# A conditioned block kernel: the opening's first slot tile reordered, slot transposes in two accumulators, the last half tile in quarters

## The chip, the cores and the metric

The kernel runs on one core of one Trainium2 chip. A core has TensorE (matmuls, here PE, with its weight loads as PEld), VectorE (DVE), ScalarE (ACT), GpSimd (POOL) and SyncE (SP, which issues most of the DMAs). The metric is the device time in microseconds of one execution, as the median of several. A profile of one execution shows when each instruction ran, on which engine, from which line of the kernel.

## The reference

The input x has 32 batch rows of 128 tokens with 512 features, in float32. A vector t per batch row (512 values) gives six modulation vectors through two linear layers after a SiLU: shift, scale and gate for each half. m marks the masked tokens, a few of each batch row.

```python
norm = _layernorm(x) * (1.0 + scale[:, None]) + shift[:, None]
norm = jnp.where(m, norm, 0.0)
fwd = _ssm_fallback(norm, ssm_w1, ssm_b1, ssm_w2, ssm_b2)
bwd = jnp.flip(_ssm_fallback(jnp.flip(norm, axis=1), bwd_w1, bwd_b1, bwd_w2, bwd_b2), axis=1)
x = x + gate_msa[:, None] * jnp.where(m, fwd + bwd, 0.0)
ff_norm = _layernorm(x) * (1.0 + scale_mlp[:, None]) + shift_mlp[:, None]
return x + gate_mlp[:, None] * (gelu(ff_norm @ ff_w1 + ff_b1) @ ff_w2 + ff_b2)
```

The first half (`_ssm_fallback` is two linear layers with an exact gelu between) matters only for the tokens that m marks. The second half is a feed-forward layer, 512 to 1024 to 512, for all tokens.

## The kernel before

**First half.** The marked tokens are gathered into 512 slots, four tiles of 128 (0 to 3). `slots_to_count` (lines 250 to 255) and `counted` (257 to 270) turn the mask into token numbers: TensorE multiplies a pick matrix with ranks, DVE compares and sums. Tiles 0 and 1 are gathered early by POOL, tiles 2 and 3 later (`gather_slots`, 289). `pm_ss` (628) receives the shift and scale rows of all batch rows from 32 matmul records as `ada_w` arrives; `modulation_rows` (318) copies them to `mod1` with DVE. `of_slots` (322 to 341) then forms the rows of each slot: four strips of 128 features, each in a PSUM accumulator of its own, with matmuls that use 32 rows of the array. Before, one call (634) makes the strips of tiles 0 and 1 in the same four accumulators. `modulated_by_strips` (343 to 354) normalises a slot tile with four DVE instructions for mean and scale, and four for the root and the shift. `transposed_slots` (189 to 196) transposes the tile by four TensorE transposes into one accumulator and two ScalarE copies of half each; it is called for slot tile 0 (682), tile 1 (691), and, back to back, tiles 2 and 3 (828 to 829). `hidden_of_tile` (666 to 680, matmuls at line 673) is the first layer for one tile and `hidden` (198) for two; `gates_of_slots` (356) makes the gate strips, and `project` (214, matmuls at 221) is the second layer.

**PSUM accumulators.** They come from three pools that reuse their buffers in turn: `ps_t` (tag "tr", two), `ps_h` (tag "h", three), `ps_o` (tag "o", three). A new tile waits until the last reader of the one two (or three) allocations back is done.

**Order.** From line 436 on the order on every engine is that in which the program issues its instructions; nothing reorders them. TensorE also multiplies things that nobody reads, into `pm_keep_clock`, to stay busy: `keep_clock(2, 0)` (635) and two matmuls on the first tile's scaled rows (646 to 649).

**Loads.** SP issues the weights and the raw x tiles in one queue: `ada_w` first, then `ssm_w1`, `bwd_w1`, two x tiles (`load_raw`, 599), `ssm_w2`, `ff_w1` and the rest. DVE takes statistics of the raw x tiles (`own_statistics`, 166) between the slot work, from line 778.

**Second half.** `FirstProduct` and `SecondProduct` do the feed-forward layer with seven products of half-size blocks in place of eight, over four pairs of 4 + 4 batch rows. The last step of the last pair (`SecondProduct.step`, 1286 to 1345, branch `last`) makes the last half of the last output tile: two token blocks (i) of 128 rows by 256 columns, each with its four matmuls into a "tr" accumulator, a multiplication by the gate and an addition to x on DVE, and a store by SP. After it come only the tests whether more slots are needed (1573 on; the loop behind them isn't entered with these inputs) and the final waits.

Of the kernel before, what the change touches and what calls it, by code (L numbers as in the profile page):

```python
# [9 lines left out]
F32 = mybir.dt.float32  # L10
# [12 lines left out]
def kernel(  # L23
# [49 lines left out]
    nc = tc.nc  # L73
    B, S, D = x.shape
    P = 128
    assert S == P
    G = 4
    NP = B // (2 * G)
    KC = D // P
# [3 lines left out]
    NH = NS // 2  # L83
    NC = NS // P
# [104 lines left out]
    def transposed_slots(xn, dst, name):  # L189

        ptr = ps_t.tile([P, 512], F32, tag="tr", name=f"ptr_{name}")
        for k in range(KC):
            nc.tensor.transpose(ptr[:, ts(k, P)], xn[:, ts(k, P)], ident)
        for half_no in range(2):
            k = ts(half_no, KC // 2)
            nc.scalar.copy(dst[:, k], ptr.rearrange("p (k s) -> p k s", s=P)[:, k])
# [53 lines left out]
    def slots_to_count(picked, n, name, bank):  # L250

        pl = bank[0].tile([P, 512], F32, tag=bank[1], name=f"pl_{name}")
        for c in range(n):
            nc.tensor.matmul(pl[:, ts(c, S)], picked[:B, ts(c, P)], rank, start=True, stop=True)  # L254
        return pl[:, : n * S].rearrange("p (c s) -> p c s", s=S)
# [28 lines left out]
    xc = []  # L284
# [33 lines left out]
    def modulation_rows(pm, mod, lo, hi):  # L318
        view = pm[:, : (hi - lo) * P].rearrange("p (m c) -> p m c", c=P)
        nc.vector.tensor_copy(mod[:, lo:hi], view)  # L320
# [140 lines left out]
    for j, op in enumerate((ALU.is_gt, ALU.is_ge)):  # L461
        nc.gpsimd.affine_select(
            out=upper[:, j],
# [167 lines left out]
    slots_of_late = slots_to_count(pick[:, NH:], NC // 2, "s1", (ps_h, "h"))  # L631
    modulation_rows(pm, mod1, 0, 2)

    strips = of_slots(pick, (0, 1), mod1, slice(0, 2), 3 * [(ps_o, "o")] + [(ps_h, "h")], "part_s0")
    keep_clock(2, 0)
# [4 lines left out]
    for c in range(2):  # L640
        mv, rstd = statistics(xc[c : c + 1], f"s{c}")
        xn_s.append(
            modulated_by_strips(xc[c], strips, c, xn[:, c], mv[:, 0, 0:1], rstd, xn[:, 2 + c])
        )
        if c == 0:
            for n in range(2):
                nc.tensor.matmul(
                    pm_keep_clock[:, ts(n, 2 * P)], ident, xn[:, 2, ts(n, 2 * P)], start=True, stop=True
                )
            token_i = counted(slots_of_late, slot_col[:, NC // 2 :], NC // 2, "s1", ssm)  # L650
# [31 lines left out]
    transposed_slots(xn_s[0], xT_s[:, :, ts(0, P)], "s0")  # L682
# [542 lines left out]
    class SecondProduct:  # L1225
# [60 lines left out]
        def step(self, step, late=False):  # L1286
# [12 lines left out]
            for i in range(2):  # L1299
                part = bank[:, ts(i, D // 2)]  # L1300
                if last:
                    part = ps_t.tile([P, 512], F32, tag="tr", name=f"last_{i}")[:, : D // 2]
                for k in range(hh):
                    nc.tensor.matmul(  # L1304
                        part,
                        src[:, k, ts(i, P)],
                        w[product][:, k, :],
                        start=(last and k == 0),
                        stop=True,
                        skip_group_check=True,  # L1310
                    )
                if last:

                    t = tp.tile([P, D // 2], F32, tag="t", name=f"t_last_{i}")
                    gate = self.gate[1][:, 2 * c + i, : D // 2]
                    nc.vector.tensor_tensor(t, part, gate, ALU.mult)
                    xt = self.xs[1][c][:, i, : D // 2]
                    nc.vector.tensor_tensor(xt, xt, t, ALU.add)
                    nc.sync.dma_start(out[(2 * p + 1) * G + 2 * c + i, :, : D // 2], xt)
# [371 lines left out]
```

## Time and profile before

| | before |
|---|---|
| median of 3 runs | 456.0 us (455.75 to 456.08) |
| the profiled execution's own time | 455.45 us |
| span of the profile | 453.7 us |
| TensorE busy | 446.6 us, 98% |
| VectorE busy | 331.7 us, 73% |
| ScalarE busy | 178.0 us, 39% |
| GpSimd busy | 159.8 us, 35% |
| mean granted TensorE clock | 0.999 |

The span runs from the first to the last instruction; the profiled execution's own time has 1.75 us around it. In a line of the timeline stand the start, the duration, the engine, the line of the kernel, the operation, output<-inputs, the number of instructions merged into the line, and in brackets how long the engine stood idle before and what released it. A float32 matmul appears as two records. The ends of matmuls are modelled, since they overlap in the array.

### The profile page before, as it was taken

How to read it: one execution, taken by the hardware profiler on the slowest of the kernel's cores; microseconds unless marked ns; L12 is line 12 of the kernel's file. 1: busy time of each engine (PE TensorE's matmuls, PEld its weight loads, DVE VectorE, ACT ScalarE, POOL GpSimd, SP SyncE). 2: the span in 40 equal slices, each digit the busy share in tenths (PEclk: the TensorE clock that was granted, in tenths of full speed). 3: DMA queues.
4: the chain of work that ended last, by engine and by line, in shares of the span. 5: the costliest groups of instructions: out<-in, count | busy, mean ns of one | idle time of the engine just before them, and what ended most of it. 6: DMA issues, size and time to landing. Idle time of an engine off the chain costs nothing.

```text
span 453.7 us, 6170 instructions
## 1 busy us (share of the span) xinstructions
PE 446.6 (98%) x2151; PEld 370.4 (82%) x2151; DVE 331.7 (73%) x571; ACT 178.0 (39%) x390; POOL 159.8 (35%) x154
## 2 busy tenths in 40 slices
PE   8999999999999999999999999999999999999996
PEld 3884585688888888888888888888888888888885
DVE  5798797697789759886796498867963995534645
ACT  3124127244642552446425514454355154552000
POOL 4220550089770000797700007977000027560000
PEclk9999999999999999999999999999999999999999
DMA  7999449745518817722187167221872442222023
GB/s 251 379 396 407 150 73 326 279 151 172 189 78 180 114 49 251 249 92 82 66 191 107 56 230 264 95 84 54 202 105 59 157 145 82 81 94 93 0 82 107
DMA packets 82611, 70.57 MB, mean 156 GB/s; under 512 B 63112, under 2 KB 63728, under 8 KB 81554
## 3 DMA queue, kind: packets, MB, share of 16 engines
q1 hardware_dynamic: 67762, 58.28, 40.9%
q0 software_dynamic: 4160, 10.54, 6.9%
q10 hardware_dynamic: 10656, 1.33, 2.1%
q8 instruction: 18, 0.29, 0.2%
q14 instruction: 15, 0.12, 0.1%
HBM read 56.46 MB, written 13.70 MB: 155 GB/s over the span
## 4 chain that ended last, share of the span: by engine, by line
PE 92%; DVE 5%; POOL 1%; issue 1%; ACT 1%; DVEq 0%
PE a_o L1304 23%; PE a_m L1117 18%; PE e_o L1304 18%; PE e_m L1117 14%; PE po_s L221 6%; PE ph_s L204 5%; PE ph_s L673 2%; PE pm_ss L309 1%; PE last L1304 1%; PE pm_f L309 1%; PE a_m_alone L1117 1%; PE pl_s L254 1%; DVE xn_sy L1050 0%; PE part_s L333 0%; DVE e_m L1142 0%
## 5 line engine op out<-in xcount | busy, mean ns | idle before, releaser
L1168 POOL TENSOR_TENSOR ha<-p_m,ha 128x512 f32<-128x512 f32 x20 | 25.8, 1289 | 178.8 <-ACT ha L1175 169.2
L1304 PE MATMUL e_o<-fw,ha 128*128 128x256 f32 x256 | 57.9, 379 | 0.0
L939 ACT ACTIVATE xT<-xT,modT 128x128 f32<-128x128 f32 x112 | 44.1, 480 | 31.6 <-DMA xT<-xn 31.4
L1304 PE MATMUL a_o<-t,hb 128*128 128x256 f32 x240 | 54.1, 379 | 0.0
L1304 PEld LDWEIGHTS e_o<-fw,ha 128*128 128x128 f32 x256 | 48.6, 190 | 6.6
L1304 PEld LDWEIGHTS a_o<-t,hb 128*128 128x128 f32 x240 | 45.6, 190 | 6.2
L1079 ACT ACTIVATE hb<-hb,biasT 128x256 f32<-128x256 f32 x64 | 29.0, 500 | 30.4 <-POOL hb L1201 19.8
L1131 ACT COPY p_m<-e_m 128x512 f32<-128x512 f32 x27 | 15.8, 586 | 47.8 <-PE e_m L1117 43.3
L885 POOL DMA_INDIRECT x<-x_rows,slot_i x24 | 29.2, 1218 | 6.0 <-issue 5.3
L1168 POOL TENSOR_TENSOR hb<-p_m,hb 128x512 f32<-128x512 f32 x20 | 29.6, 1481 | 0.3
L1304 PE MATMUL a_o<-fw,ha 128*128 128x256 f32 x128 | 28.9, 379 | 0.0
L1304 PE MATMUL a_o<-t,s 128*128 128x256 f32 x128 | 28.9, 379 | 0.0
L1304 PE MATMUL e_o<-fw,s 128*128 128x256 f32 x128 | 28.9, 379 | 0.0
L221 PE MATMUL po_s<-w,h_s 128*128 128x512 f32 x64 | 28.4, 594 | 0.0
L1175 ACT COPY ha<-e_m 128x512 f32<-128x512 f32 x32 | 18.5, 578 | 24.9 <-PE e_m L1117 24.6
L1304 PEld LDWEIGHTS a_o<-t,s 128*128 128x128 f32 x128 | 24.3, 190 | 3.3
L1304 PEld LDWEIGHTS a_o<-fw,ha 128*128 128x128 f32 x128 | 24.3, 190 | 3.3
L1304 PEld LDWEIGHTS e_o<-fw,s 128*128 128x128 f32 x128 | 24.3, 190 | 3.3
L1142 DVE TENSOR_TENSOR e_m<-a_m,ha 128x512 f32<-128x512 f32 x20 | 13.9, 696 | 17.0 <-POOL ha L1168 6.6
L1079 ACT ACTIVATE ha<-e_m,biasT 128x256 f32<-128x256 f32 x48 | 20.0, 468 | 14.8 <-PE e_m L1117 12.6
L1117 PE MATMUL a_m<-xT,tw 128*128 128x256 f32 x96 | 24.7, 380 | 0.4 <-DVE hb L1147 0.4
L1117 PE MATMUL e_m<-s,fw 128*128 128x256 f32 x92 | 23.8, 381 | 0.0
(237 smaller groups left out, 892.3 us busy)
## 6 DMA issues: line engine op xcount, KB each, us to landing
tw<-t_rows SPq DMA_DIRECT2D x16, 896.0 KB, 5.3
x<-in_x_dram SPq DMA_DIRECT2D x16, 512.0 KB, 8.8
gate<-gate_rows POOLq DMA_DIRECT2D x8, 1024.0 KB, 5.2
out_dram<-x SPq DMA_DIRECT2D x15, 512.0 KB, 4.9
xT<-xn SPq DMA_DIRECT2D x92, 64.0 KB, 2.4
ada_f<-in_L_cond_ffada_w_dram SPq DMA_DIRECT2D x4, 768.0 KB, 13.2
ada_a<-in_L_cond_ada_w_dram SPq DMA_DIRECT2D x4, 512.0 KB
w<-in_L_cond_ssm_w_dram SPq DMA_DIRECT2D x2, 1024.0 KB, 6.2
```

Source lines behind the costliest of these rows:

```text
L204: nc.tensor.matmul(ph[:, :n], w[:, k, ts(f, P)], xT[:, k, :], start=(k == 0), stop=(k == KC - 1))
L221: nc.tensor.matmul(po, h[f][:, ts(i, P)], w[:, f, :], start=(f == 0 and seeded is None), stop=(f == HC - 1), skip_group_check=seeded is no ...
L309: nc.tensor.matmul(pm[ts(j, B), : (hi - lo) * P], sT[:, k, :], kinds[:, k, lo:hi, ts(j, P)], start=False, stop=True, skip_group_check=True,)
L885: nc.gpsimd.indirect_dma_start(out=xs[i // G][i % G // 2][:, i % 2], out_offset=None, in_=x1_rows, in_offset=bass.IndirectOffsetOnAxis(ap= ...
L939: nc.scalar.activation(out, src, AF.Identity, bias=shift, scale=scale)
L1079: nc.scalar.activation(dst[:, n], src[:, n], AF.Gelu_apprx_tanh, bias=biasT[:, f : f + 1])
L1117: nc.tensor.matmul(bank[:, ts(n, QT)], self.w_block(j, product)[:, ts(n, P)], self.x_block(j, product), start=(product in ("P1", "P5") and ...
L1131: nc.scalar.copy(p5, e)
L1142: nc.vector.tensor_tensor(e, a, p5, add)
L1168: nc.gpsimd.tensor_tensor(self.place(RESULT[j], c), self.p5[j], other, ALU.add)
L1175: nc.scalar.copy(self.place(RESULT[j], c), src)
L1304: nc.tensor.matmul(part, src[:, k, ts(i, P)], w[product][:, k, :], start=(last and k == 0), stop=True, skip_group_check=True,)
```

## The change

Five edits:

- `modulation_rows` for the shift and scale rows (632) is replaced by a ScalarE copy.
- The strips of slot tiles 0 and 1 are made by two calls. Tile 0's come between the two matmuls of the late slot count (`between`), tile 1's after tile 0's transposes. `modulated_slots(0)`, the transposes of tile 0 and the strips of tile 1 now stand ahead of `counted`, and the transposes ahead of the gathers in the program.
- The matmuls into `pm_keep_clock` are halved: `keep_clock(1, 0)` and one matmul on the scaled rows.
- `transposed_slots` uses two "tr" accumulators for a tile, two transposes and one copy for each. This holds for all its calls.
- In the last step the second token block is made in two quarters of 128 columns: four matmuls, two DVE operations and a store for each.

```diff
     def transposed_slots(xn, dst, name):
-        ptr = ps_t.tile([P, 512], F32, tag="tr", name=f"ptr_{name}")
-        for k in range(KC):
-            nc.tensor.transpose(ptr[:, ts(k, P)], xn[:, ts(k, P)], ident)
         for half_no in range(2):
-            k = ts(half_no, KC // 2)
-            nc.scalar.copy(dst[:, k], ptr.rearrange("p (k s) -> p k s", s=P)[:, k])
+            ptr = ps_t.tile([P, 512], F32, tag="tr", name=f"ptr_{name}_{half_no}")
+            for n in range(2):
+                nc.tensor.transpose(ptr[:, ts(n, P)], xn[:, ts(2 * half_no + n, P)], ident)
+            nc.scalar.copy(
+                dst[:, ts(half_no, KC // 2)], ptr[:, : 2 * P].rearrange("p (k s) -> p k s", s=P)
+            )
...
-    def slots_to_count(picked, n, name, bank):
+    def slots_to_count(picked, n, name, bank, between=None):
         pl = bank[0].tile([P, 512], F32, tag=bank[1], name=f"pl_{name}")
         for c in range(n):
+            if c and between:
+                between()
             nc.tensor.matmul(pl[:, ts(c, S)], picked[:B, ts(c, P)], rank, start=True, stop=True)
...
     modulation_matmuls(pm, ada_a, 0, 2, range(KC))
-    slots_of_late = slots_to_count(pick[:, NH:], NC // 2, "s1", (ps_h, "h"))
-    modulation_rows(pm, mod1, 0, 2)
-
-    strips = of_slots(pick, (0, 1), mod1, slice(0, 2), 3 * [(ps_o, "o")] + [(ps_h, "h")], "part_s0")
-    keep_clock(2, 0)
+    strips_of = {}
+
+    def parts_of_tile(c):
+        strips_of[c] = of_slots(
+            pick, (c,), mod1, slice(0, 2), 3 * [(ps_o, "o")] + [(ps_h, "h")], f"part_s{c}"
+        )
+
+    nc.scalar.copy(mod1[:, 0:2], pm.rearrange("p (m c) -> p m c", c=P)[:, 0:2])
+    slots_of_late = slots_to_count(
+        pick[:, NH:], NC // 2, "s1", (ps_h, "h"), lambda: parts_of_tile(0)
+    )
+    keep_clock(1, 0)
...
-    for c in range(2):
+
+    def modulated_slots(c):
         mv, rstd = statistics(xc[c : c + 1], f"s{c}")
         xn_s.append(
-            modulated_by_strips(xc[c], strips, c, xn[:, c], mv[:, 0, 0:1], rstd, xn[:, 2 + c])
-        )
-        if c == 0:
-            for n in range(2):
-                nc.tensor.matmul(
-                    pm_keep_clock[:, ts(n, 2 * P)], ident, xn[:, 2, ts(n, 2 * P)], start=True, stop=True
-                )
-            token_i = counted(slots_of_late, slot_col[:, NC // 2 :], NC // 2, "s1", ssm)
+            modulated_by_strips(xc[c], strips_of[c], 0, xn[:, c], mv[:, 0, 0:1], rstd, xn[:, 2 + c])
+        )
+
+    modulated_slots(0)
+    nc.tensor.matmul(pm_keep_clock[:, : 2 * P], ident, xn[:, 2, : 2 * P], start=True, stop=True)
+    transposed_slots(xn_s[0], xT_s[:, :, ts(0, P)], "s0")
+    parts_of_tile(1)
+    token_i = counted(slots_of_late, slot_col[:, NC // 2 :], NC // 2, "s1", ssm)
+    modulated_slots(1)
     gather_slots(token_i)
...
-    transposed_slots(xn_s[0], xT_s[:, :, ts(0, P)], "s0")
     ptr = ps_t.tile([P, 512], F32, tag="tr", name="ptr_b")
...
-            for i in range(2):
-                part = bank[:, ts(i, D // 2)]
+            whole = 0, D // 2
+            for i, (lo, hi) in ((0, whole), (1, (0, P)), (1, (P, 2 * P))) if last else ((0, whole), (1, whole)):
+                part = bank[:, i * D // 2 + lo : i * D // 2 + hi]
                 if last:
-                    part = ps_t.tile([P, 512], F32, tag="tr", name=f"last_{i}")[:, : D // 2]
+                    part = ps_t.tile([P, 512], F32, tag="tr", name=f"last_{i}_{lo}")[:, : hi - lo]
                 for k in range(hh):
                     nc.tensor.matmul(
                         part,
                         src[:, k, ts(i, P)],
-                        w[product][:, k, :],
+                        w[product][:, k, lo:hi],
...
-                    t = tp.tile([P, D // 2], F32, tag="t", name=f"t_last_{i}")
-                    gate = self.gate[1][:, 2 * c + i, : D // 2]
+                    t = tp.tile([P, hi - lo], F32, tag="t", name=f"t_last_{i}_{lo}")
+                    gate = self.gate[1][:, 2 * c + i, lo:hi]
                     nc.vector.tensor_tensor(t, part, gate, ALU.mult)
-                    xt = self.xs[1][c][:, i, : D // 2]
+                    xt = self.xs[1][c][:, i, lo:hi]
                     nc.vector.tensor_tensor(xt, xt, t, ALU.add)
-                    nc.sync.dma_start(out[(2 * p + 1) * G + 2 * c + i, :, : D // 2], xt)
+                    nc.sync.dma_start(out[(2 * p + 1) * G + 2 * c + i, :, lo:hi], xt)
```

## The prediction

> **What bounds the kernel now.** The page was read first: the engines' busy time, then the chain of work that ended last.
>
> ```profile
> span 453.7 us, 6170 instructions
> PE 446.6 (98%) x2151; PEld 370.4 (82%) x2151; DVE 331.7 (73%) x571; ACT 178.0 (39%) x390; POOL 159.8 (35%) x154
> PE 92%; DVE 5%; POOL 1%; issue 1%; ACT 1%; DVEq 0%
> ```
>
> TensorE is busy for 446.6 of 453.7 us and 92% of the chain is its own. So an edit counts only where it moves a moment at which TensorE stands still or starts: a saving elsewhere is worth nothing, and a new TensorE wait goes to the end in full. There are four such places; the timeline shows each (starts of single records, below, are from narrower windows of it). First, the opening:
>
> ```profile
> 11.46 0.93 PE L254 MATMUL pl_s<-rank,pick 32*128 32x128 f32 x3
> 11.60 0.42 DVE L320 COPY mod<-pm_ss 128x256 f32<-128x256 f32 x1 [2.12 <-PE pm_ss L309]
> 11.94 0.68 DVE L158 BATCH_NORM_STATS2 st_s<-xc 128x6 f32<-128x512 f32 x1
> 12.09 0.52 PE L333 MATMUL part_s<-mod,pick 32*128 32x256 f32 x3
> 13.41 1.12 DVE L347 SCALAR_TENSOR_TENSOR xn_s<-xc,mv_s,part_s 128x128 f32<-128x128 f32 x4 [0.38 <-PE part_s L333]
> 14.45 1.12 DVE L351 SCALAR_TENSOR_TENSOR xn_s<-xn_s,rstd_s,part_s 128x128 f32<-128x128 f32 x4
> 15.27 0.69 PE L193 MATMUL ptr_s<-ident,xn_s 128*128 128x128 f32 x4
> 15.99 0.65 ACT L196 COPY xT_s<-ptr_s 128x256 f32<-128x256 f32 x2 [8.80 <-PE ptr_s L193]
> 16.46 3.81 PE L673 MATMUL ph_s<-xT_s,w 128*128 128x128 f32 x32 [0.27 <-issue]
> ```
>
> The modulation row must be copied (DVE, to 12.02) before the strips (part_s) are multiplied. DVE waits for all sixteen strip records, which end at 13.37, though the first tile needs only eight. Then come two passes over four strips, four transposes, a copy, and the first hidden matmul at 16.46. Second, the gates of the slots; third, the transposes of the two late slot tiles:
>
> ```profile
> 25.80 0.68 DVE L171 BATCH_NORM_STATS2 st_x<-x 128x6 f32<-128x512 f32 x1
> 33.89 0.34 DVE L351 SCALAR_TENSOR_TENSOR x<-x,rstd_s,part_s 128x128 f32<-128x128 f32 x1
> 34.17 0.60 PE L333 MATMUL gate_s<-mod,pick 32*128 32x128 f32 x9
> 35.43 0.70 PE L221 MATMUL po_s<-w,h_s 128*128 128x512 f32 x1
> ```
>
> ```profile
> 49.27 1.04 PE L193 MATMUL ptr_s<-ident,x 128*128 128x128 f32 x8
> 50.23 0.58 PE L296 MATMUL pm_f<-modb,quarter 4*128 4x384 f32 x1
> 49.90 0.37 ACT L196 COPY xT_s<-ptr_s 128x256 f32<-128x256 f32 x1 [5.92 <-PE ptr_s L193]
> 50.17 0.38 ACT L196 COPY xT_s<-ptr_s 128x256 f32<-128x256 f32 x1
> ```
>
> The fourth gate strip uses the accumulator of the strip that DVE reads until 34.23, so the gates finish just behind DVE. The eight late transposes run without a break, since each tile fills one of the two "tr" accumulators. Last, the end:
>
> ```profile
> 445.75 3.62 PE L1304 MATMUL last<-t,hb 128*128 128x256 f32 x16
> 449.40 0.42 DVE L1316 TENSOR_TENSOR t_last<-last,gate 128x256 f32<-128x256 f32 x1 [0.84 <-PE last L1304]
> 449.86 0.42 DVE L1318 TENSOR_TENSOR x<-x,t_last 128x256 f32<-128x256 f32 x1
> 450.31 0.34 SPq L1319 DMA_DIRECT2D out_dram<-x  x1
> ```
>
> From that store's issue to the end of the span is 3.4 us, which no part of the change shortens.
>
> **Opening, up to the first hidden matmul.** The copy of the row goes to ScalarE: 0.37 us, as its copies of 128x256 from PSUM take at 15.99, for DVE's 0.42; ready at 11.97 instead of 12.02. ScalarE has been idle since 7.2, so nothing is queued behind it. DVE now heads for the statistics of the first tile and waits there only for its gather: issued at 6.95, 4.4 us to landing, 11.35. So statistics run 11.4 to 12.5 and the root on POOL (0.58) to 13.2; nothing that others need is queued on DVE behind that wait. TensorE multiplies only four strips (eight records) ahead of the second count. In the trace a strip's two records start 0.36 apart and the last takes 0.38: 12.04 + 0.36 + 0.38 = 12.78, so DVE starts its first pass near 12.82 instead of 13.41, a gain of 0.59. Its ends follow: last pass over at 14.97 instead of 15.57.
>
> From there TensorE's own order counts. Transposes of strips 3 and 4 start by 15.03, then the four strips of tile 1 stand in front of the hidden layer, where before they were done by 13.37. Their price: a gap of 0.20 on changing from full to 32-row matmuls (25.78 to 25.98 in the trace), two records 0.32 apart, about 0.2 until the bias transposes can start, 0.09 between these, and 0.09 more: hidden begins near 15.03 + 0.20 + 0.32 + 0.20 + 0.09 + 0.09 = 15.93. It has another guard: its accumulator is now the one that holds the late count, which DVE leaves 0.59 earlier than before (16.54), at 15.95, plus 0.05 for the wait. I take 16.05 against 16.43 (first weight load): a gain of 0.38. Bounds: 0.55 if neither guard holds, and a loss of 0.1 if the parts of tile 1 cost as much as the whole sixteen records did (1.28). The keep-warm matmuls that go (eight records of L620, two of L647) stood in waiting time and free nothing.
>
> **What is left of it.** The late gathers leave POOL about 0.6 earlier, since the second tile's root does. DVE is continuously busy from 22.20 (released by TensorE) to 34.23 and could run 0.38 earlier, but at 25.80 it takes the second x load, issued at 14.53 with 11.0 us to landing: 25.5. So at most 0.25 passes. The gathers, at 6.6 and 6.9 us to landing, share the DMA engines with that load, so their earlier start can only push it later: 25.5 to 25.8, a gain of 0.25 to 0. I take the middle, 0.12. TensorE arrives 0.38 earlier at the gates and waits for DVE's last strip. Kept from the opening: **-0.12** (bounds -0.38, were the load early, to +0.1).
>
> **The late transposes.** The diff changes a helper that is also called for slot tiles 2 and 3, back to back. Now each takes two accumulators, of which there are two; so the first pair of tile 3 must wait for ScalarE's copy of the first pair of tile 2, a wait that does not exist now. Pairs of tile 2 start at 49.27 and 49.49, the second matmul 0.11 later, ending 0.27 after that: 49.65 and 49.87. Copies: 49.69 to 50.06 and, 0.27 behind it as in the fence, 49.96 to 50.33. Tile 3's pairs then start at 50.11 and 50.39 (0.05 for the wait, as from 15.57 to 15.62 in the opening) and the last transpose at 50.49; before it started 0.20 ahead of pm_f, at 50.03. Behind it on TensorE stand pm_f and all the rest: **+0.46** (bounds +0.3, were the wait free and copies 0.05 faster each, to +0.55). Earlier arrival of TensorE does not help, as ScalarE's copies are timed by TensorE. In the opening its two accumulators let the first copy start early, which the count above does not need, as the other guards end later; for tile 1 the accumulator it needs is that of the bias columns, read by DVE's cast at 19.53 (18.9 after), well before 19.9.
>
> **The end.** The second half, one set of eight records at 0.216, becomes two sets of eight at 0.111 (the pace at L673): 1.78 for 1.73, last end 449.43 instead of 449.38. DVE's two steps on 128 columns: the 128x127 operation at L260 takes 0.29, so 449.45, 449.77, over at 450.06. The store leaves at 450.09 instead of 450.31. The extra store's issue (0.34, at most the 0.78 that the previous store took) begins near 449.37 and is out by 450.15 at worst. **-0.20** (bounds -0.25 and 0: the wait of one more semaphore at the end, or the extra issue in the way). The data of the last store move between 451.1 and 451.7, while SP walks through its final waits until 452.7; so a faster or slower transfer is covered by some 0.3 us, and beyond that counts.
> The Trainium skill, DMA: Bandwidth & Descriptors, section Bandwidth, says that stores should be batched and that transfers below 64 KB are dominated by descriptors; it lists 0.95 us of transfer for 64 KB. The trace moves 128 KB in about 0.5 us. By the page, which speaks against quarters, the last piece would land some 0.4 us later than by the row, and the end term would be about -0.1 instead of -0.20.
>
> **Sum.** -0.12 + 0.46 - 0.20 = +0.14. The profiled execution took 455.45 us (span 453.7 and 1.75 around it), 0.55 under the median of the runs shown; its own sum is 455.6, and on the median **456.0 + 0.14, about 456.1 us**. 0.2% is 0.91 us, about what a measurement of this kernel can tell from no change. The likeliest case's own range, by its bounds, is 455.6 to 456.6.
>
> **Rivals.**
> - The late wait does not appear, as though copies were out of the way: -0.12 - 0.20, 455.7; with the whole 0.38 of the opening kept, 455.4. Against it: two accumulators and four uses in a row.
> - Faster by over 0.2%: the whole 0.59 of DVE's earlier start reaches the end, the x load lands 0.3 earlier, the late wait is hidden and the end gives 0.25, with 0.1 from the gates (whose fourth strip lost 0.15 waiting): -0.94, 455.05. Three covers must fail at once.
> - Slower, by the second x load: the gathers now overtake it. Each microsecond that it lands beyond 25.5 delays DVE, the gates and TensorE by as much. The gather landing last now, at 19.66 + 6.6 = 26.3, bounds it: +0.75. The sum is then -0.25 + 0.75 + 0.46 - 0.20 = +0.76, 456.8; it passes 0.2% from a landing at 26.4.
> - Slower, by the clock: half of the keep-warm work goes, and a granted clock at half speed for about 3 us of the first hidden stage costs 1.5 us: 457.6. For it: the clock falls to 0.50 in the last microsecond of the span. Against it: it fell some 3 us after the last matmul, and no gap in the changed opening is over 0.6; it decides only if one nears 3.
>
> **How the numbers follow.** Forecast 55%, no late wait 14%, faster 11%, late load 9% (half of it beyond 0.2%), clock 11%. Faster 0.11, within 0.2% 0.73, slower 0.16. The range leaves out most of the clock case and about half of the faster one: 455.1 to 457.0.
>
> **What the profile after would show.** L347 of the first tile near 12.8 with the statistics already done; L673 near 16.1; DVE's second x statistics at 25.5 to 25.8; the eight late transposes over some 1.5 us with a wait for ScalarE, and pm_f 1.4 us behind their first instead of 0.96; the last store issued 0.2 us earlier against the last half's first matmul. Wrong would be: no wait at the late transposes, the gates' DVE strips earlier by over 0.3 us, or granted clock below 1 in the opening.

## The result and the profile after

| | before | after |
|---|---|---|
| median (lowest to highest), 6 runs each | 455.88 us (455.19 to 456.31) | 458.45 us (457.79 to 459.58) |
| ratio, with its 95% interval | 1 | 1.0061 (1.0045 to 1.0076) |
| profiled execution's own time | 455.45 us | 458.45 us |
| span of its profile | 453.7 us | 456.7 us |

The change makes the kernel 0.6% slower, 2.6 us by the medians. The forecast was 456.1 us with a range of 455.1 to 457.0, so it was wrong: the sign was right and the size was not.

The page of the changed kernel, first the engines, then the chain that ended last by engine:

```profile
span 456.7 us, 6171 instructions
PE 447.2 (98%) x2149; PEld 370.1 (81%) x2149; DVE 331.1 (72%) x572; ACT 178.7 (39%) x391; POOL 160.2 (35%) x154
PE 65%; DVE 12%; SPq 7%; ACT 5%; DMA 4%; issue 3%; POOL 3%; ACTq 0%; DVEq 0%; POOLq 0%
```

TensorE's work has hardly grown (447.2 us after 446.6). But the chain no longer runs along TensorE for 92%: it passes through SP's queue, DMA, ScalarE and VectorE. Those engines now hold TensorE up somewhere in the middle of the kernel, which no step of the prediction spoke of. The opening of the changed kernel, from its timeline:

```profile
11.77 0.71 PE L336 MATMUL part_s<-mod,pick 32*128 32x256 f32 x8
12.50 1.12 DVE L350 SCALAR_TENSOR_TENSOR xn_s<-xc,mv_s,part_s 128x128 f32<-128x128 f32 x4 [0.68 <-PE part_s L336]
13.54 1.12 DVE L354 SCALAR_TENSOR_TENSOR xn_s<-xn_s,rstd_s,part_s 128x128 f32<-128x128 f32 x4
13.94 1.10 PE L194 MATMUL ptr_s<-ident,xn_s 128*128 128x128 f32 x4
14.97 0.71 PE L336 MATMUL part_s<-mod,pick 32*128 32x256 f32 x8
16.16 2.02 PE L685 MATMUL ph_s<-xT_s,w 128*128 128x128 f32 x16 [0.40 <-DMA w<-in_L_cond_ssm_w_dram]
...
25.49 0.69 DVE L171 BATCH_NORM_STATS2 st_x<-x 128x6 f32<-128x512 f32 x1
...
33.86 1.34 PE L336 MATMUL gate_s<-mod,pick 32*128 32x128 f32 x32
```

VectorE starts its first pass at 12.50 instead of 13.41, the hidden layer at 16.16 instead of 16.46, held up here by its weight load, and the gates come 0.3 us earlier. The late transposes, where ScalarE's copy of the first pair now stands before tile 3's first pair:

```profile
48.97 0.60 PE L194 MATMUL ptr_s<-ident,x 128*128 128x128 f32 x4
49.39 0.65 ACT L195 COPY xT_s<-ptr_s 128x256 f32<-128x256 f32 x2 [5.70 <-PE ptr_s L194]
49.81 0.71 PE L194 MATMUL ptr_s<-ident,x 128*128 128x128 f32 x4 [0.24 <-ACT xT_s L195]
50.46 0.91 PE L299 MATMUL pm_f<-modb,quarter 4*128 4x384 f32 x2
```

And the end, where VectorE's last two steps are short and the last of three stores is issued at 452.03 (the line merges the three):

```profile
450.51 1.85 SPq L1331 DMA_DIRECT2D out_dram<-x  x3
451.38 0.29 DVE L1328 TENSOR_TENSOR t_last<-last,gate 128x128 f32<-128x128 f32 x1 [0.28 <-PE last L1316]
451.71 0.29 DVE L1330 TENSOR_TENSOR x<-x,t_last 128x128 f32<-128x128 f32 x1
```

From 452.03 to the end of the span it is 4.69 us, where it was 3.42.

To see where the time came in, each TensorE record of the changed kernel was set beside the same record of the profile before, and the difference of their starts followed through the span. It is -0.30 us from the hidden layer to 45 us, +0.23 after the late transposes (a step of 0.53), +0.78 from 183 us on, +0.72 from there to 355, and +1.93 from 367 us to the last half tile. The last records end with +2.09, the last store is issued 0.96 us after the last record's start instead of 1.33, and the tail adds 1.27:

-0.30 + 0.53 + 0.49 + 1.21 + 0.16 - 0.37 + 1.27 = +2.99 us, the 3.0 us between the two spans (in this order: opening, late transposes, the steps up to 355 us, the step from 355 to 367 us, the longer last matmuls, the earlier store, the tail). Opening, late transposes and the gain at the end are in the prediction; the steps at 183 and at 355 to 367 us and the longer tail are not.

### The profile page after: what moved, and what is told of

Read it like the earlier page. It is cut to its first block, busy times and chain, and to the rows that moved or that the text cites. A ratio compares the mean times of both kernels' runs of the same rounds, so it can differ in the third digit from the quotient of the medians.

```text
span 456.7 us, 6171 instructions
## 1 busy us (share of the span) xinstructions
PE 447.2 (98%) x2149; PEld 370.1 (81%) x2149; DVE 331.1 (72%) x572; ACT 178.7 (39%) x391; POOL 160.2 (35%) x154
## 3 DMA queue, kind: packets, MB, share of 16 engines
q10 hardware_dynamic: 10656, 1.33, 2.1%
## 4 chain that ended last, share of the span: by engine, by line
PE 65%; DVE 12%; SPq 7%; ACT 5%; DMA 4%; issue 3%; POOL 3%; ACTq 0%; DVEq 0%; POOLq 0%
PE a_m L1128 15%; PE e_m L1128 13%; PE a_o L1316 11%; PE e_o L1316 9%; SPq L967 7%; PE po_s L222 6%; PE ph_s L205 5%; ACT xT L950 3%; DMA xT<-xn 3%; DMA w<-in_L_cond_ssm_w_dram 2%; PE ph_s L685 2%; DVE t_o L1289 1%; DVE sx L1057 1%; DVE s L997 1%; DVE x L1291 1%
## 5 line engine op out<-in xcount | busy, mean ns | idle before, releaser
L1179 POOL TENSOR_TENSOR ha<-p_m,ha 128x512 f32<-128x512 f32 x20 | 25.8, 1289 | 180.7 <-ACT ha L1186 170.6
L950 ACT ACTIVATE xT<-xT,modT 128x128 f32<-128x128 f32 x112 | 44.1, 479 | 34.5 <-DMA xT<-xn 32.9
L1142 ACT COPY p_m<-e_m 128x512 f32<-128x512 f32 x27 | 15.8, 586 | 45.5 <-PE e_m L1128 39.7
L1090 ACT ACTIVATE ha<-e_m,biasT 128x256 f32<-128x256 f32 x48 | 20.0, 469 | 15.8 <-PE e_m L1128 14.7
L1158 DVE TENSOR_TENSOR hb<-a_m,hb 128x512 f32<-128x512 f32 x20 | 13.7, 685 | 14.4 <-PE a_m L1128 14.3
```

The lines of the kernel that those rows point to most:

```text
L950: nc.scalar.activation(out, src, AF.Identity, bias=shift, scale=scale)
L1090: nc.scalar.activation(dst[:, n], src[:, n], AF.Gelu_apprx_tanh, bias=biasT[:, f : f + 1])
L1142: nc.scalar.copy(p5, e)
L1179: nc.gpsimd.tensor_tensor(self.place(RESULT[j], c), self.p5[j], other, ALU.add)
```

## The experiments

All profiles in one table. Columns two to six: TensorE's offset against the profile of before, at these times of it; then the last store's issue after the start of the last TensorE record, and the end of the span after that issue; the start of VectorE's code read near 330 us, which the text comes to; and the time at which TensorE's records become short.

| kernel | 16.5 | 45 | 50.6 | 340 | 367 | store | end | read | fast from |
|---|---|---|---|---|---|---|---|---|---|
| before | 0 | 0 | 0 | 0 | 0 | 1.33 | 3.42 | 328.8 | 12.1 |
| before_again | -0.25 | -0.23 | -0.23 | -0.21 | -0.31 | 1.33 | 3.42 | 328.5 | 11.8 |
| before_20_fewer | +0.23 | +0.23 | +0.23 | +0.28 | +0.50 | 1.33 | 3.43 | 329.1 | 12.7 |
| before_row_by_act | -0.55 | -0.41 | -0.41 | +0.32 | +0.67 | 1.33 | 3.42 | 336.9 | 11.1 |
| before_quarters | +1.61 | +1.62 | +1.62 | +1.64 | +1.55 | 0.96 | 4.31 | 330.3 | 15.5 |
| after | -0.30 | -0.30 | +0.23 | +0.72 | +1.93 | 0.96 | 4.69 | 337.1 | 11.1 |
| after_again | -0.21 | -0.18 | +0.34 | +0.52 | +0.55 | 0.96 | 4.31 | 336.9 | 12.9 |
| after_20_more | -0.77 | -0.30 | +0.22 | +0.99 | +2.22 | 0.96 | 4.33 | 337.1 | 10.7 |
| own_accumulator | +0.91 | +0.93 | +1.45 | +3.79 | +4.98 | 0.96 | 5.05 | 340.1 | 16.8 |
| late_whole | -0.63 | -0.04 | -0.04 | 0.00 | +1.47 | 0.95 | 4.33 | 336.6 | 12.0 |
| row_by_dve | +0.76 | +0.85 | +1.37 | +1.38 | +1.36 | 0.96 | 4.44 | 330.1 | 16.6 |
| no_quarters | -0.85 | -0.07 | +0.45 | +0.50 | +1.76 | 1.33 | 3.42 | 336.8 | 11.4 |
| one_store | -0.76 | +0.08 | +0.60 | +0.95 | +2.25 | 0.96 | 4.12 | 337.5 | 11.6 |
| one_more_dve | +0.55 | +0.59 | +1.11 | +1.45 | +1.54 | 0.96 | 4.44 | 330.2 | 15.9 |
| after_warm | +1.63 | +1.66 | +2.19 | +3.14 | +4.65 | 0.96 | 4.43 | 339.6 | 16.5 |
| three_undone | -0.67 | -0.64 | -0.64 | +0.30 | +0.28 | 1.33 | 3.42 | 329.0 | 11.9 |
| three_undone_warm | +1.69 | +1.72 | +1.72 | +1.74 | +1.52 | 1.33 | 3.42 | 330.7 | 16.5 |

### The late transposes by themselves

```diff
-        transposed_slots(xn_late[c], xT_t[:, :, ts(c, P)], f"s{2 + c}")
+        transposed_whole(xn_late[c], xT_t[:, :, ts(c, P)], f"s{2 + c}")  # one accumulator, as before
```

> The changed kernel with the transposes of slot tiles 2 and 3 in one accumulator for a tile, as before. By the prediction's step the wait for ScalarE goes and TensorE is 0.46 to 0.51 us earlier from 50 us on. Theory 'by itself': that is all, 457.95. Rival 'late phase': the delays at 183 and 365 us (another 1.7 us of TensorE) come because this wait put TensorE behind the other engines; then they go too, and the time is 456.3.

457.61 us, ratio 1.0039 (1.0021 to 1.0058). The step between 45 and 50.6 us is 0.00; in all nine profiles with the transposes in two accumulators it is 0.52 or 0.53. The step at 355 to 367 us stays (1.47). So the wait costs its 0.5 us and has nothing to do with the rest: "by itself" holds, "late phase" falls.

### The code reads

The trace records, beside the data, reads of program code: 16 KB at a time for TensorE, about every 26 us, and 8 KB at a time for the other engines. Each read is one packet, and so on one DMA engine, while a data transfer lands in sixteen parts. A code read lies at a point of an engine's instruction stream, so an edit anywhere ahead of it can move it. First, TensorE's own stream, 20 instructions shorter in the opening. In the kernel before one of its reads starts at 136.9 us, ahead of the turn transfers (`xT<-xn`, 64 KB each, issued by SP, by which the normalised tiles of the second half are brought into transposed order); in the changed kernel it starts at 140.3, and the issue by SP at 140.53 takes 1.39 us instead of 0.63.

```diff
-    on_zeros(512, 512, 512, 512)
+    on_zeros(512, 512, 512, *11 * [32])                  # after_20_more
...
-    keep_clock(2, 0)
+    keep_clock(1, 0)                                      # before_20_fewer, and one matmul on the scaled rows fewer
```

> The changed kernel with ten more matmuls of 32 columns on zeros at the very start, in time in which TensorE waits: 20 instructions of TensorE, as many as the opening lost with the keep-warm matmuls. Theory 'code reads': TensorE's code arrives in reads of 16 KB, about every 26 us; where one falls on a turn transfer's issue by SP, that issue takes 1.4 to 1.5 us instead of 0.63. Twenty instructions shift the reads back to where they are in the kernel before (136.9 instead of 140.3): the issues near 140 take 0.6 to 0.7 us again, TensorE's delays at 183 and 365 us shrink from 1.7 to 0.3 or so, and the time is about 457.1. Rival 'the edits': the delays come from the edits' own timing; the time stays at 458.45.

> The kernel before without the ten records of keep-warm matmuls that the change drops, and nothing else: 20 instructions of TensorE fewer. Theory 'code reads': the reads of code move later to where the changed kernel has them (140.3 instead of 136.9), the turn transfer's issue there takes 1.4 us, and the time grows by 0.6 to 1.4 us, to 456.5 to 457.3, with no edit on any engine's path. Rival 'the edits': 455.9, within 0.2.

The reads moved as expected (137.9 in the one, 140.4 in the other). The time did not follow: 457.65 us, ratio 1.0036 (1.0023 to 1.0049) for the first, with other steps in place of the one at 183 us; 456.22 us, ratio 1.0004 (0.9994 to 1.0014) for the second, where 0.6 to 1.4 us were expected. That TensorE's reads alone explain the extra time falls, though `after_20_more`, which keeps everything that is found below, is 0.8 us below the changed kernel's median. In its profile the 0.78 us between 51 and 183 us is for the most part a wait of TensorE at 119 us for the load `tw<-t_rows`. That wait is in five of the seventeen profiles, in neither of the changed kernel's two, and why the load is late was not tested. Of the profiles with the read at 140 to 141 us, three have a step of 0.4 to 0.6 us at 183, and six have none.

Second, VectorE's stream. At 336.6 to 337.1 us the profiles of the changed kernel, of `late_whole` and of `after_20_more` have an 8 KB read among the turn transfers, which the profile of before has at 328.8. That it is VectorE's goes by the instruction counts: in all seventeen profiles it starts after the 572nd or 573rd of VectorE's recorded instructions or after the 578th, while the read next to it, at 332 to 334 us in most, stays at the 208th or 209th of SP's. Of the transfer that SP issued at 334.49, fifteen of sixteen parts landed between 336.95 and 338.04, the last at 339.19 only; SP's issue at 339.20 waits for it. SP's waits between 335 and 345 us, in the changed kernel:

```profile
SPq L967 <- DMA xT<-xn: 1.5, 1, 1.5
SPq L1295 <- DVE x L1291: 0.8, 1, 0.8
```

By this wait of 1.5 us SP's later turn issues, ScalarE's scaling of the turned tiles (L950, which waits 3.8 us for the transfers, and 2.7 in `one_more_dve` below) and VectorE's sums (L997) come later, and TensorE is held up between 355 and 367 us, where it waits for VectorE. TensorE's waits in the changed kernel, over the whole span (the first line is not among the prediction's steps, 0.5 of its 0.8 us fall between 355 and 369 us and 0.3 at 183; the second line, 0.7 us, is in the kernel before too):

```profile
PE e_m L1128 <- DVE e_m L1172: 0.8, 2, 0.5
PE a_m L1128 <- DVE hb L1158: 0.7, 2, 0.4
PE ph_s L685 <- DMA w<-in_L_cond_ssm_w_dram: 0.4, 1, 0.4
PE ptr_s L194 <- ACT xT_s L195: 0.2, 1, 0.2
```

VectorE has one instruction fewer there, the copy of the modulation row that went to ScalarE. Three kernels test it: the copy put back, the copy alone moved in the kernel before, and one unread instruction more with the copy left on ScalarE.

```diff
-    nc.scalar.copy(mod1[:, 0:2], pm.rearrange("p (m c) -> p m c", c=P)[:, 0:2])
+    modulation_rows(pm, mod1, 0, 2)                       # row_by_dve
...
-    modulation_rows(pm, mod1, 0, 2)
+    nc.scalar.copy(mod1[:, 0:2], pm.rearrange("p (m c) -> p m c", c=P)[:, 0:2])   # before_row_by_act
...
+    unread = const.tile([P, 1], F32, name="unread")       # one_more_dve
+    nc.vector.memset(unread, 0.0)
     nc.scalar.copy(mod1[:, 0:2], pm.rearrange("p (m c) -> p m c", c=P)[:, 0:2])
```

> The changed kernel with the modulation row copied by VectorE, as before, and all else changed. Theory 'code of VectorE': in the three profiles of kernels with the copy on ScalarE an 8 KB read of code falls at 336.6 to 337.1 us, among the turn transfers, which then land on one DMA engine at 339.2 where the other engines are done at 337.0; in the two profiles with the copy on VectorE it falls at 328.8 and 329.1, and nothing waits. VectorE has then executed 578 and 573 instructions: the copy that went from its stream shifted the read. With the copy back, the read returns to 329, the issue by SP at 339.2 comes 1.2 us earlier, TensorE's step of 1.2 us between 355 and 367 us shrinks to 0.2, and the time falls by about 1.0, to 457.4. Rival 'the other edits': the step stays, and the time stays at 458.4 (the copy itself is worth 0.05).

> The kernel before with one edit: the modulation row is copied by ScalarE instead of VectorE. Theory 'code of VectorE': one instruction fewer on VectorE moves its 8 KB code read from 328.8 to 337 us, between the turn transfers; TensorE's step of about 1.2 us at 355 to 367 us appears, and the time is about 457.0. Rival 'the other edits': the copy costs 0.05 less on the opening's path, and the time is 455.9.

> The changed kernel with one more VectorE instruction: a memset of one column that nobody reads, while VectorE waits for the first gather. The copy of the row stays on ScalarE. Theory 'count of VectorE's instructions': the place of its 8 KB code read depends on how many instructions stand before it, so the read goes from 337 back to 329, TensorE's step between 355 and 367 us falls from 1.2 to under 0.3, and the time falls by about 1.0, to 457.4, as with the copy back on VectorE. Rival 'ScalarE's copy': the step comes from ScalarE's own stream or from the copy's timing; then the read stays at 337 and the time at 458.4.

`row_by_dve`: 457.29 us, ratio 1.0029 (1.0006 to 1.0051). `one_more_dve`: 457.55 us, ratio 1.0025 (1.0011 to 1.0040). In both the read is back at 330 us, and the step between 340 and 367 us is -0.02 and +0.09 where the changed kernel has 1.21. With one memset that nobody reads the ratio is 1.0025 instead of 1.0061. The medians alone do not settle it, since `after_20_more` has the read at 337.1 and the step of 1.23, and its 1.0036 cannot be told from 1.0025; the steps in the profiles carry the argument. SP's waits between 335 and 345 us in `one_more_dve`; its first line, a wait to store an output, does not reach TensorE by 367 us, where the step is 0.09:

```profile
SPq L1297 <- DVE x L1293: 1.9, 1, 1.9
SPq L969 <- DMA xT<-xn: 0.4, 1, 0.4
```

So it is the number of VectorE's instructions ahead of the read, not the copy's engine. Why one instruction moves the read by five or six, from the 573rd to the 578th, the count does not say, nor why a read of 0.31 us (337.13 to 337.44) makes a part land 1.15 us late. `before_row_by_act` moves the read to 336.9 as expected, but its step there is only 0.35; its 456.7 us, ratio 1.0008 (0.9991 to 1.0024), cannot be told from no change. The second profile of the changed kernel shows the same:

> The changed kernel once more, one look. VectorE's code read falls at 337 us plus the shift of the run, TensorE's step between 355 and 367 us is 1.0 to 1.5 us, the wait at the late transposes 0.5, and the end comes 4.1 to 5.1 us after the last store's issue; the hidden layer starts at 15.6 to 16.2, or near 17.3 where TensorE stays slow.

The read is at 336.9, but the step is 0.03, and this execution took 456.7 us; its other steps came as expected (0.52 at the late transposes, 4.31 at the end). In both, transfers behind the read land late on one engine as well, but the one for which SP waits had just landed (337.8 instead of 338.7 to 339.5 in the five other profiles with the read between 336.6 and 337.5). The read costs 1.2 to 1.5 us where it catches that transfer, as in seven of nine profiles, and 0.0 or 0.35 where it does not. All eight profiles with the read at 328 to 331 us have between -0.22 and +0.22.

### The end

In the changed kernel fifteen of the last store's sixteen parts have landed 1.57 us after its issue, the sixteenth lands 3.0 us after it; before, all had landed after 1.75. Two causes were set against each other: packets of 512 bytes, or a code read on the same DMA engine. After its last matmul TensorE loads a register and jumps over the loop that isn't entered, and a read of 16 KB follows, 1.1 to 2.7 us after the jump in all seventeen profiles. That it is the code beyond the jump is inferred from this. TensorE's sequencer runs ahead of the array: before, the jump is at 446.22 and the read at 447.3, 3.0 us ahead of the last store. In the changed kernel the jump is at 451.35 and the read at 453.0, 1 us behind the store's issue.

```diff
-                    part = ps_t.tile([P, 512], F32, tag="tr", name=f"last_{i}_{lo}")[:, : hi - lo]
+                    pool, tag = (ps_h, "h") if lo else (ps_t, "tr")           # own_accumulator
+                    part = pool.tile([P, 512], F32, tag=tag, name=f"last_{i}_{lo}")[:, : hi - lo]
...
-            for i, (lo, hi) in ((0, whole), (1, (0, P)), (1, (P, 2 * P))) if last else ((0, whole), (1, whole)):
+            for i, (lo, hi) in ((0, whole), (1, whole)):                      # no_quarters
...
-                    nc.sync.dma_start(out[(2 * p + 1) * G + 2 * c + i, :, lo:hi], xt)
+                    if hi == 2 * P:                                           # one_store: whole rows of 256
+                        nc.sync.dma_start(out[...][:, : 2 * P], self.xs[1][c][:, i, : 2 * P])
```

> The changed kernel, with the third piece of the last half tile in an accumulator of tag h in place of the third use of the two tr accumulators. Theory 'late jump': in the changed kernel this piece's first weight load waits until VectorE has read the first block (450.03); TensorE's instruction stream stands there, so that its jump over the unused loop comes at 451.35 instead of 446.2, and the 16 KB read of its code at 453.0 instead of 447.3, beside the last store, which lands 3.0 us after its issue instead of 1.75. Without the wait the jump comes by 448, the code read by 449.5, the last store lands 1.75 us after its issue, and from its issue to the end of the span it is 3.4 us instead of 4.7: about 1.3 us less than the changed kernel's 458.45, 457.2. Rival 'small store': packets of 512 bytes land late by themselves; then the store still takes 3.0 us and the time stays at 458.45.

> The changed kernel with the last half tile as before: two pieces of 256 columns, two stores. By the prediction's step the last store is issued 0.2 us later against the last half's first matmul. From its issue to the end it is 3.4 us, as before, instead of 4.3 to 5.1 in the changed kernel's relatives, if the quarters made the tail longer, by either theory ('late jump' or 'small store'): the time falls by 0.7 to 1.1, to 457.4 to 457.7. If the tail has another cause, the time rises by 0.2.

> The changed kernel with the matmuls and VectorE's steps of the second block in quarters, but one store of 256 columns for both, so that the last store has packets of 1024 bytes as before. Theory 'late jump': TensorE's instructions are the same, its jump over the unused loop still comes at the end and its 16 KB code read beside the last store; the store lands 2.5 to 3.0 us after its issue, and from issue to end it is 4.3 to 4.7 us. Rival 'small store': with packets of 1024 bytes it lands 1.75 us after its issue and the end comes 3.4 us after it, 0.9 to 1.3 us less than the changed kernel.

> The kernel before with the last half tile in quarters and nothing else. Theory 'late jump': the last store is issued 0.96 us after the last matmul record's start instead of 1.33 (a gain of 0.2 after the longer matmuls), TensorE's jump comes at the end, its 16 KB code read stands beside the last store, and the end comes 4.1 to 4.7 us after that store's issue instead of 3.4: 0.5 to 1.1 us slower, 456.5 to 457.1. By the prediction's step it would be 0.2 faster, 455.8.

`no_quarters`: 457.20 us, ratio 1.0012 (0.9993 to 1.0031), and the end 3.42 us after the last store's issue. `one_store`: 458.05 us, ratio 1.0051 (1.0021 to 1.0082): with packets of 1024 bytes the end still comes 4.12 us after the issue, and the last part lands 2.78 us after it. That leaves the code read. The DMA engines' busy shares between 452 and 455 us (40 equal slices, in tenths) and the queues, first the changed kernel, then `no_quarters`:

```profile
DMA  7994000000028951000000000000101000000000
q1 hardware_dynamic: 300, 0.14, 16.4%
q8 instruction: 1, 0.02, 2.0%
```

```profile
DMA  0000000000005899861000000000000000000000
q1 hardware_dynamic: 151, 0.14, 13.6%
```

In the first the last store's packets are done on most engines by 453.2. A code read lasts from 453.04 to 453.99, and the trace's packets show what stands behind it: the store's last eight of 512 bytes, one after the other from 453.97 on (the ones at 454). In the second no code read falls there and nothing trails. Seven profiles without quarters all have 3.42 or 3.43 us from store to end; the ten with the second block in quarters have 4.12 to 5.05. `before_quarters` shows the same alone: 0.96 and 4.31 in place of 1.33 and 3.42, which with 0.16 us more of matmuls is +0.7. Its median is 456.83 us, its ratio 1.0004 (0.9985 to 1.0024), so the whole time does not settle it; its opening fell late (+1.6) in the profile.

`own_accumulator` was to bring the jump forward. It did by half: the register load starts 2.1 us ahead of the last TensorE record instead of 1.0. But the code was read at 455.3, 0.2 us behind the last store's issue, and the end came 5.05 us after it; 459.64 us, ratio 1.0073 (1.0053 to 1.0093). So the reused accumulator is not the main reason. (Its last part landed 2.74 us after the issue, much as in the others; another 0.6 of the 5.05 us come after that landing and are not explained.) The register load stands 16 weight loads ahead of the end there, as in the kernel before. At 0.216 us each they hide 3.5 us, at the quarters' 0.111 only 1.8. That the read then also starts 2.7 us after the jump instead of 1.1 (1.7 in the changed kernel), with the stores before it on the queues, is seen but not explained.

### The sum, and the keep-warm work

```diff
+    modulation_rows(pm, mod1, 0, 2)                                  # three_undone: the row by VectorE,
+        transposed_whole(xn_late[c], xT_t[:, :, ts(c, P)], ...)      # late transposes in one accumulator,
+            for i, (lo, hi) in ((0, whole), (1, whole)):             # two pieces at the end
...
+    keep_clock(2, 0)                                                 # the warm kernels: ten records put back
```

> The changed kernel with three parts undone: the row copied by VectorE, the transposes of slot tiles 2 and 3 in one accumulator for a tile, the last half tile in two pieces. What is left is the opening's new order and its ten keep-warm records fewer. Theory 'three causes': late transposes 0.5, VectorE's code read 1.0 to 1.2 and the tail 0.9 to 1.3 (less 0.2) make up the changed kernel's 2.6 us; without them the step at 50 us is 0, the step at 355 to 367 us under 0.4, the end comes 3.4 us after the last store's issue, and the time is 455.7 to 456.3, or 456.7 in executions in which TensorE stays at its slow pace until 16.9 us. Rival 'a fourth cause': the time stays above 457.

> The same with the ten keep-warm records of the kernel before put back in the opening. Theory 'slow pace': TensorE starts at half its pace (a record of 256 columns 634 ns instead of 379) and becomes fast between 10.7 and 12.7 us in eight of ten profiles, but at 16.9 in two, both with the shortened keep-warm work; with the work back it becomes fast by 13.5 at the latest, the hidden layer starts at 15.6 to 16.5, and the time is 455.4 to 455.8, with less spread than without. Rival 'no effect': the same time as without the ten records, within 0.2, and a start at 17.2 still occurs.

> The changed kernel with the ten keep-warm records put back, nothing else. By theory 'slow pace' the opening is never late (hidden layer at 15.7 to 16.2), 0.3 less than the changed kernel in the mean. They also put back 20 instructions of TensorE, with which its code read near 140 us moves back to 137 to 138. Late transposes, VectorE's code read and the tail stay: 457.6 to 458.2. Rival: 458.45, no difference.

> The kernel before once more, one look. TensorE's change from its slow to its fast pace fell at 12.0 us in its first profile. If the moment is a matter of the execution and not of the kernel, it will fall at another time between 10.6 and 17 us, and TensorE's first hidden weight load moves with it, between 15.7 and 18.2.

`three_undone` takes 455.77 us, ratio 0.9986 (0.9966 to 1.0006). Undoing the three causes removes the whole loss; what the opening's new order alone gives cannot be told from no change.

The theory that the keep-warm work brings the end of the slow pace forward fell. TensorE's records are long at first (634 ns for 256 columns instead of 379) and become short at some moment. With the ten records put back that moment was 16.5 us in both profiles, not 13.5 at the latest, and `before_quarters`, whose opening is that of the kernel before, has 15.5. A late moment moves the hidden layer by +0.55 to +0.91 us with the shortened keep-warm work and by +1.6 to +1.7 with the whole, as the long records then stand in the way. Medians: `three_undone_warm` 456.25 us, ratio 1.0000 (0.9979 to 1.0021), `after_warm` 458.02, ratio 1.0037 (1.0014 to 1.0060). The second profile of the kernel before had 11.8 instead of 12.1, which moved the hidden layer to 16.2 as the expectation allows, but is too small a difference to tell its two cases apart. The trace's own clock records say what changes: the first one, at full clock, begins at 12.19 us in the profile before, 11.14 in the changed kernel, 15.88 in `before_quarters`, 16.92 in `own_accumulator`, and in all seventeen within 0.4 us of the last column. Ahead of it there is no record, and a row that says 1.00 there is empty, not measured. An opening with a late moment, from `own_accumulator`; four strips take 1.23 us where the changed kernel's profile has 0.71:

```profile
11.84 1.23 PE L336 MATMUL part_s<-mod,pick 32*128 32x256 f32 x8
13.41 1.08 PE L623 MATMUL pm_keep_clock<-ada_a,sT 128*32 128x256 f32 x8
14.42 1.22 PE L658 MATMUL pm_keep_clock<-xn_s,ident 128*128 128x256 f32 x2
17.37 0.38 PE L685 MATMUL ph_s<-xT_s,w 128*128 128x128 f32 x1
```

## Why the prediction was wrong

- **Opening: right in size, but only against a like moment of the clock.** The prediction's rows span the change of pace at 12.19 us, which it did not see, and that moment alone moves the first hidden matmul: in kernels with the old order it starts at 15.91 where full clock comes at 11.09 (`before_row_by_act`), and at 16.46 where it comes at 12.19. Where it comes between 11.9 and 12.2, the old order has 16.21 and 16.46, the new one 15.79 and 15.83 (`three_undone`, `late_whole`): a gain of 0.4 to 0.6 for the predicted 0.38. In the changed kernel's first profile, with full clock at 11.14, part is luck. The first pass was predicted at 12.82 and came at 12.50, since the accumulation ended 0.25 us earlier and TensorE was fast by then. The first hidden weight load was predicted at 16.05 and came at 16.13, behind its weights' landing at 16.02; in the relatives with full clock by 12.02 it comes at 15.6 to 15.8. The guard named (VectorE leaving the late count at 15.95) fell earlier, at 15.64; by the prediction's own terms it gave 16.00, so 0.05 of the 16.05 has no source.
- **"What is left of it": not refuted, too small to be seen.** Predicted -0.12 (bounds -0.38 and +0.1), with VectorE's second x statistics at 25.5 to 25.8. Measured at 45 us: -0.30 and -0.18 in the two profiles of the change, and -0.30 to +0.08 in its relatives with an early fast pace (three_undone, at -0.64, is outside). In those the statistics start at 25.49 to 25.87, in three_undone at 25.16. `after_20_more` shows the mechanism: -0.77 at the hidden layer, -0.30 at the gates. But the kernel before has -0.23 there in its own second profile, and `before_row_by_act`, with the old order, -0.41, so a gain of 0.12 is within what one execution differs from another.
- **Late transposes: right.** Predicted +0.46, measured 0.52 or 0.53.
- **End: wrong.** The failing sentence is "From that store's issue to the end of the span is 3.4 us, which no part of the change shortens". It was not asked whether a part lengthens it. The earlier issue is there (0.37 us nearer to the last record, which itself is 0.16 later: the predicted -0.20), but the tail grew by 0.7 to 1.6, so the term is +0.7 and +1.1 in the two profiles of the change, +0.5 to +1.4 with its relatives. The prediction looked for the covered time in the store's own data, and not in what TensorE does after its last matmul. The Trainium skill, DMA: Bandwidth & Descriptors, section Bandwidth, which asks for large batched transfers, gave no better answer; its 0.95 us for 64 KB is a row of loads issued by GpSimd. Here, without the code read, by fifteen of its sixteen parts, the piece of 64 KB landed 1.57 us after its issue, and the one of 128 KB, by all of them, 1.75 us.
- **The copy on ScalarE: a term was missing.** It was costed at 0.37 for 0.42 us and a row ready 0.05 earlier, which is right where it stands (0.37 us at 11.35). That it takes an instruction out of VectorE's stream had no price. It is the largest single one of the first profile: 1.2 us where the moved read catches SP's transfer, nothing where it just misses it.
- **Rivals.** The clock case was the nearest: TensorE at a slower pace, though ahead of the first hidden stage and not in it, not because the keep-warm work was halved, and with 0.5 to 0.9 us in place of 1.5. A late moment happens with both openings, and in neither of the two profiles that the account compares. The sign that was named for it, a granted clock below 1 in the opening, could not appear, as the trace has no clock record there. The late x load did not occur in the two profiles of the change (statistics at 25.49 and 25.61), nor did the case without a late wait. The late load was also given half its chance beyond 0.2%, which its own bound of +0.75 does not reach.
- **The sum.** -0.12, +0.46 and -0.20 made +0.14. By the profiles the terms are -0.3 to +0.1, +0.5, and at the end +0.7 to +1.1, and beside them 0 to 1.5 for VectorE's read. Medians, each against its own runs of the kernel before, agree only roughly: the change is 2.57 us slower, the kernels with one cause undone 1.67 (late transposes), 1.01 (the copy; 1.37 by the memset) and 0.92 us (the end), with all three undone -0.16. The single undoings sum to 3.8 to 4.1 us, more than the 2.7 of all three, so a single size is good to about half a microsecond. The step at 183 us (0.5 in the first profile, none in the second) stays open, as do the other steps between 112 and 300 us, which are not all small: 0.9 at 119 us in `three_undone`, 1.5 between 274 and 287 us in `own_accumulator`.

## What to carry to other kernels

When an edit adds or removes an instruction, it can also move later code reads of that engine, and a read that falls among transfers for which a queue waits can cost more than the edit's own terms. So look in the trace where the code reads lie against tight transfers, and test a suspicion with one unread instruction. At an end, count what every engine does after its last useful instruction: a jump whose code is read beside the last store is on the path, and shorter matmuls hide less of it. A helper that takes two buffers for one must be priced at each of its calls, also those far from the edit.

## What the runs showed of the hardware

- A code read holds one DMA engine: TensorE's 16 KB for 0.9 to 2.1 us, the other engines' 8 KB for 0.3 to 0.8. One part of a transfer that meets it then lands 0.8 to 1.4 us after the other fifteen (in the changed kernel 339.19 after 338.04, 455.04 after 453.60). At the end it is the same engine, as the late packets start at 453.97 where the read ends at 453.99; at 337 us that is inferred. Turn issues by SP that a 16 KB read falls on mostly take 1.0 to 2.3 us instead of 0.63; the kernel before has two such (at 245.7 and 328.5 us). The Trainium skill, Runtime: NRT & Kernel Launch, section Instruction fetch mechanics, says that instruction memory is refilled in blocks of 16 KiB while the engine works, at a cost that is mostly hidden, and that a taken branch breaks the prefetch. The trace agrees for TensorE's blocks and for the read after the jump; the other engines' reads are of 8 KB. TensorE's waits shown above hold none for a regular block; the cost falls on transfers that share the DMA engine.
- TensorE multiplies from 1.25 us on, but its records become short only between 10.7 and 12.9 us in eleven of seventeen profiles and between 15.5 and 16.8 in six, in kernels with the same opening too. At the slow pace records of 256 columns start 0.42 us apart, at the fast one 0.21: half speed. The first clock record of the trace, at 1.00, begins within 0.4 us of the change in all seventeen, and there is none ahead of it; it lasts 436.9, 440.3 or 443.7 us, values 3.4 us apart, and is followed by one at 0.50. The Trainium skill, TensorE: Matmul & The Clock Gate, section Part 1, describes half speed until a free-running window of 3.4 us has been busy. The two paces and the steps of 3.4 us are there; that the change comes 9 to 16 us after the first matmul, no run here explains.
